# Four graph layers in FP32: first loads on one queue, identity products moved behind adj x, no warming products, planned times anew

## The chip, the cores and the metric

The kernel runs on one core of a Trainium2 chip. A core has five engines that each work through their own instructions in order and wait for one another by semaphores: PE (TensorE, matrix products), DVE (VectorE), ACT (ScalarE), POOL (GpSimd) and SP (SyncE), which here issues DMA transfers. The metric is the device time of one execution in microseconds (us). The profile comes from one execution that was recorded by the hardware profiler.

## The reference

The input x has 128 graphs of 128 nodes with 512 features, and adj is one 128x128 matrix. Four layers follow each other, each with a residual sum and a layer norm over the features. Cut to what matters:

```python
# layer 0
y = einsum('nm,bmd->bnd', adj, x);  x = norm(x + y @ w0 + bias0)
# layer 1
q, k, v = x @ Wq.T, x @ Wk.T, x @ Wv.T
rel = adj.T * einsum('bnd,bmd->bnm', q, k)
rel = rel / norm2(rel, axis=2);     x = norm(x + rel @ v)
# layer 2
h = x @ W;  e = leaky_relu(h @ a1 [:, :, None] + h @ a2 [:, None, :]) * adj
att = softmax(e);                   x = norm(x + elu(att @ h + beta * h))
# layer 3: both of its weights are adj, so that it needs max over d of (adj x), and b
A = einsum('od,bdn->bon', adj, x);  x = norm(x + relu(max(A, -1) + b))
```

All of it is in 32-bit floats.

## The kernel before, in words

**Tiling.** The 128 graphs are taken in 32 groups of four (G = 4, NG = 32). A group's x is one tile of 128 nodes by 4 by 512. Each group goes through `layer0` to `layer3`, and the groups overlap: while one is in layer 0, the group before is in layer 1 and an older one in layers 2 and 3.

**The names on PE.** Layer 0: `p_y` is adj x for one graph (four products of 128x128 into a PSUM bank, each two instructions in the records[...]), which ACT copies into yT. `r_y` is the product of yT with w0. Layer 1: `p_xT` transposes x, `r_m` multiplies it by m_qk (Wq and Wk were multiplied into one matrix at the start, `r_qk`), DVE adds the result up in tT, `p_rel` is tT times xT, `r_v` the product with Wv (transposed at the start by `p_wv`), `p_o` the product with the normed rel. Layer 2: `p_z` gathers by the attention, `r_z` multiplies by the weight. Layer 3: `p_a` is adj x again. `wa` makes rows of the weight times a, once.

**The four weighted products.** `product` replaces a 2x2 block product by seven block products (numbers 1 to 7). They need sums of blocks: POOL makes those of the left operand (`left_factors`: s_y, s_x, s_q), DVE makes those of the weight once (`weight_blocks`: t_0, t_k, t_m, t_v, t_2). The seven go into three PSUM regions: 1, 6, 7 and 4 share bank r0, 2 has a bank of tag pi, 5 and 3 share bank r12. After each of them `out(i)` reads the region (DVE adds it to the destination, or ACT copies it), and the next one of the same region accumulates on top. From the third group on, products 2 and 4 are split once more into small ones (the rows named `pi_`).

**Bias.** For `r_y` the bias is put into the bank ahead of the products: `fill` lets ACT write `bias_sb` into regions r0 and r12, and the products accumulate on it without a start flag. So that they accumulate, each of these two banks has to have been written once by PE. Two products of the identity (`first_r`, 128x512 each, four instructions together) do this at the very start.

**What sets the order.** There is no automatic scheduler. `emit(at, f)` files a piece of work under a planned time `at`, and at the end all pieces are sorted by it and issued; every engine then keeps its program order. Pieces of the steady groups have their times in `TABLE` (a slot per group), groups 0 and 1 have exceptions in `FIRST`, the last three groups in `LAST`; `STEPS` holds the offsets of the seven products and the small ones. One-time pieces have times of their own. All that goes through the order-keeping helper has line L26 in the profile.

**The start.** SP issues adj, x_0, x_1 (of group 0, 256 KB each), bias (broadcast to all partitions), x_2, x_3, wq, wk, wv, w2, a, beta, b3, while ACT issues w0 on its own queue (L110). The later x loads of a whole group (1 MB) are pieces. PE has, in this order: first_r, p_adjT (the transpose of adj), eight products `p_warm` of the identity that nobody reads (16 instructions), the four p_y of group 0, then r_y.

The lines that the change touches first:

```python
warm = bank("p_warm")
for i in range(WARM):
    pe.matmul(warm[:, :P], ident, ident, start=True, stop=True)
```

Of the kernel before, what the change touches and what calls it, by code (L numbers as in the profile page):

```python
# [8 lines left out]
FP = mybir.dt.float32  # L9
# [20 lines left out]
def kernel(  # L30
# [32 lines left out]
    nc = tc.nc  # L63
# [10 lines left out]
    WARM = 8  # L74
# [19 lines left out]
    nc.sync.dma_start(adj_sb, adj)  # L94
    x1, x2, x3 = {}, {}, {}

    def load(g):
        x1[g] = data.tile([P, G, D], FP, tag="x1", name=f"x1_{g}", bufs=3)
        if g == 0:
            for b in range(G):  # L100
                nc.sync.dma_start(x1[g][:, b, :], x[b])
                if b == 1:
                    nc.sync.dma_start(bias_sb, on_all(bias0, D))
        else:
            sync.dma_start(x1[g], x[g * G : (g + 1) * G].rearrange("b n d -> n b d"))

    bias_sb = const.tile([P, D], FP)
    load(0)
    w0_sb = const.tile([P, K, D], FP)
    nc.scalar.dma_start(w0_sb, w0.rearrange("(k p) f -> p k f", p=P))  # L110
    wq_sb = work.tile([P, K, D], FP, tag="tv", name="wq_sb")
    nc.sync.dma_start(wq_sb, wq.rearrange("(k p) f -> p k f", p=P))
    wk_sb = work.tile([P, K, D], FP, tag="c", name="wk_sb")
    nc.sync.dma_start(wk_sb, wk.rearrange("(k p) f -> p k f", p=P))
    wv_sb = work.tile([P, K, D], FP, tag="xB", name="wv_sb")
    nc.sync.dma_start(wv_sb, wv.rearrange("(k p) f -> p k f", p=P))

    w2_sb = const.tile([P, K, D], FP)
    nc.sync.dma_start(w2_sb, w2.rearrange("(k p) f -> p k f", p=P))
    a_sb = data.tile([P, 2, D], FP, tag="x3", name="a_sb", bufs=1)  # L120
    nc.sync.dma_start(a_sb.rearrange("p s d -> p (s d)"), on_all(a2, 2 * D))
    beta_sb = const.tile([P, 1], FP)
    nc.sync.dma_start(beta_sb, on_all(beta, 1))
    b3_sb = const.tile([P, 1], FP)
    nc.sync.dma_start(b3_sb, b3.rearrange("(p o) -> p o", o=1))
# [5 lines left out]

    for tag, n in (("r0", 1), ("r12", 1)):
        for i in range(n):
            r = psum.tile([P, 2, H], FP, tag=tag, name=f"first_{tag}_{i}", bufs=n)
            pe.matmul(r, ident, ident[:, None, :].to_broadcast([P, G, P]), start=True, stop=True)
# [7 lines left out]

    warm = bank("p_warm")
    for i in range(WARM):
        pe.matmul(warm[:, :P], ident, ident, start=True, stop=True)
# [99 lines left out]
    def row(at, step, n=G):  # L246
# [4 lines left out]
        load=[-21.1232], y=[0.9608, 1.8251, 2.1487, 2.7922],  # L251
        y_sums=[4.5561, 5.0639, 6.7629, 6.9969], y_inner=[5.2833, 7.5035, 7.9599, 7.7423],
        y_w=[6.4865, 10.1067, 9.7011, 18.5098, 16.5578, 25.5346, 18.8593],
        stats0=[13.0727, 13.9676, 15.6348, 14.8804], norm0=[15.6928],
        apply0=[16.441, 16.56, 17.1055, 18.4252], turn=[16.9531, 18.9169, 15.0983, 23.7872],
        turn_blocks=[17.6387, 18.378, 19.3199, 18.8892], move=[21.2268, 20.1475, 23.7935, 24.4105],
        x_sums=[25.5484, 25.8887, 25.5714, 27.1546], x_inner=[27.0248, 27.3651, 27.6181, 27.4647],
        m=[28.2059, 29.9451, 30.7559, 39.3743, 35.0579, 32.0807, 31.5941],
        scores=[35.5574, 36.2751, 36.3095, 39.6263], masked=[40.1785], squares=[41.2658],
        turn_rel=[40.8158], move_rel=[43.2987, 45.3105, 45.5881, 44.1661], inverse=[42.7358],  # L260
        v=[41.1537, 34.8028, 35.2269, 32.9135, 36.819, 44.1908, 45.5822],
        attend=[51.1788, 52.5818, 53.9439, 54.1297], residual=[51.7575, 52.9793, 54.8472, 55.5115],
        squares1=[52.1071, 55.1681, 55.5885, 56.295], dots=[52.6394, 54.6161, 55.8601, 56.5298],
        norm1=[56.6185], scale=[58.0637], apply1=[67.3359, 67.3118, 68.311, 67.3949],
        spread=[61.4852], leaky=[62.1614], weighted=[62.3481], greatest=[63.6868], exps=[63.9389],
        divide=[64.6743], turn_att=[66.48], with_beta=[55.7842], turn_blocks_2=[65.0697],
        move_2=[65.6032], gather=[70.1205, 71.0446, 73.2368, 74.4083],
        z_sums=[74.7466, 74.9675, 75.3471, 79.5091], z_inner=[76.2873, 76.452, 76.7576, 79.7843],
        z_w=[76.5238, 78.3454, 80.9549, 82.1806, 80.3108, 74.0925, 83.986],
        exp=[84.1886, 85.0555, 95.1779, 97.9857], elu=[86.5931, 86.915, 97.0853, 99.5009],  # L270
        norm2=[100.4793], apply2=[101.1271, 102.2, 101.6434, 101.6261],
        widen=[102.9021, 104.404, 104.6097, 106.3071],
        top=[104.9696, 105.5877, 105.8825, 107.7194], norm3=[108.5946],
        apply3=[109.0064, 110.4459, 109.9895, 111.6524], store=[116.2428],
# [4 lines left out]
            y=[-0.9173, 0.2561, 2.5559, 2.6098], y_sums=[5.7842, 6.1923, 7.6412, 8.0217],  # L279
            y_w=[6.656, 6.9826, 8.5177, 10.5158, 10.5177, 12.1185, 12.1169],  # L280
            stats0=[14.8567, 15.0593, 15.0036, 15.7551], norm0=[16.1054],
            m=[26.9197, 27.6264, 27.6652, 28.2251, 29.8853, 32.0185, 32.0172],
            scores=[35.9958, 37.3155, 38.45, 39.3155], masked=[39.5575], squares=[42.4727],
            turn_rel=[41.0869], move_rel=[42.4032, 42.1994, 41.3572, 41.7949],
            v=[42.7111, 44.0451, 45.3088, 46.3784, 47.3081, 48.2976, 49.1509],
            attend=[50.3341, 51.6935, 52.7247, 53.3341],
            residual=[51.2419, 52.2419, 52.8787, 54.4537],
            squares1=[51.6342, 53.6777, 54.5661, 54.7798], norm1=[56.2059],
            apply0=[17.374, 17.6244, 18.5295, 18.0555], turn=[18.8709, 19.7935, 20.9961, 21.5866],
            dots=[55.2805, 58.6316, 60.212, 60.5925], scale=[61.2871], spread=[61.7827],  # L290
            leaky=[62.1], weighted=[62.205], greatest=[64.0362], exps=[64.0854], divide=[65.2555],
            turn_blocks_2=[65.6], move_2=[67.0921],
        ),
        1: dict(
            y=[-11.6669, -10.4156, -10.312, -9.8874], y_sums=[-3.77, -3.67, -1.551, 3.0174],
            y_w=[7.0161, 7.9774, 8.126, 9.7685, 10.9791, 11.4015, 12.7041],
            stats0=[14.0438, 14.1814, 14.7308, 15.7036], norm0=[17.4806],
            attend=[49.1976, 51.8422, 53.416, 53.4184],
            apply0=[18.4423, 19.1027, 20.4894, 18.5104], turn=[21.0277, 21.0846, 21.3846, 21.542],
            x_sums=[22.8224, 24.281, 27.507, 28.0022],  # L300
# [5 lines left out]
            exp=[0.4623, 11.611, 13.6093, 21.9374], elu=[6.6028, 13.5806, 17.1367, 22.1806],  # L306
            norm2=[23.3538], apply2=[25.0389, 27.3987, 25.9338, 25.563],
            squares3=[35.4179, 39.239, 38.0926, 41.5412],
            widen=[44.4948, 56.0663, 55.0979, 58.4343], top=[44.9981, 56.3795, 60.4284, 60.9337],
            norm3=[62.9017], apply3=[64.4412, 66.5207, 68.7228, 67.9152], store=[69],  # L310
        ),
        NG - 2: dict(
            scale=[4.3047], apply1=[4.6775, 11.0377, 10.4618, 10.2756], spread=[6.9011],
            leaky=[8.5406], weighted=[8.6149], greatest=[11.14], exps=[12.7308], divide=[14.9407],
            turn_att=[19.4796], with_beta=[20.9256], gather=[33.1448, 34.2964, 34.1197, 33.8382],
            z_sums=[37.1312, 37.1799, 37.2299, 38.9411],
            z_w=[37.2, 39.2089, 40.5339, 42.6626, 45.9385, 46.5626, 47.9032],
            exp=[51.1816, 51.9016, 53.9016, 58.1278], elu=[51.9326, 54.0745, 59.5933, 63.8365],
            norm2=[65.6683], apply2=[66.9349, 67.9136, 68.7218, 69.9541],
            widen=[72.5885, 69.738, 73.9565, 76.7205], top=[73.9072, 73.9667, 75.9682, 78.4954],  # L320
            stats3=[68.0781, 73.1502, 70.7817, 73.9103], norm3=[73.9726],
            apply3=[81.0356, 88.4294, 88.4341, 88.4354], store=[91.3384],
        ),
        NG - 1: dict(
            load_w2=[-23.6669], m=[-1.0223, 1.0487, 2.4676, 3.6749, 7.9692, 8.2221, 9.9221],
            scores=[10.4191, 11.0622, 12.0436, 13.2103], masked=[14.918], squares=[15.9336],
            turn_rel=[17.0025], inverse=[19.5602],
            v=[17.0016, 19.283, 20.9796, 22.8356, 24.6364, 26.4739, 27.9989],
            attend=[30.1034, 30.2339, 30.8373, 30.4857],
            residual=[30.4, 31.4552, 33.8743, 31.7856],  # L330
            stats1=[33.7623, 34.1537, 33.9623, 34.1488], norm1=[34.3934],
            dots=[34.3979, 35.5481, 35.1904, 40.2755], scale=[40.5527],
# [87 lines left out]
    def by_columns(p, a, b, first):  # L420

        for c in range(2):
            for k in range(2):
# [21 lines left out]
    STEPS = {  # L445
        "m": (
            {
                1: (-1.2981, -0.3541),
                6: (1.724, 2.1528),
                7: (3.0677, 3.3979),  # L450
                5: (4.5184, 5.1615),
# [822 lines left out]
```

## Time and profile before

| what | value |
|---|---|
| median of three runs | 2141.93 us (2141.5 to 2142.24) |
| the profiled execution's own time | 2141.56 us |
| its span, first to last instruction | 2139.7 us |
| mean granted clock of PE | 0.997 |
| ACT busy, share of the span | 60% |
| POOL busy, share of the span | 45% |
| DMA, mean over the span | 65 GB/s |

How to read it: the span is shorter than the execution's time by 1.9 us, which lie before the first and behind the last instruction. The busy share of an engine is an average over the start, the steady groups and the end, which can have different limits. A row of the timeline gathers neighbouring instructions of one kind: its first number is the start of the first of them, its second the time to the end of the last; the ends of PE's instructions are modelled, so that starts are the safer numbers. A group takes about 65 us (the same p_rel of two neighbouring groups starts at 954.13 and 1019.09).

### The profile page before, as it was taken

Reading aid. Unit: us, or ns where it says so; the run is one execution under the profiler, and the core shown is the slowest. Engines: PE = TensorE matmul, PEld = TensorE weight load, DVE = VectorE, ACT = ScalarE, POOL = GpSimd, SP = SyncE. Lnnn points to the kernel's source line nnn. Section 1 sums busy time; section 2 is a strip of 40 time slices with the busy share of each in tenths; the row PEclk is TensorE's granted clock in tenths of the full one; section 3 lists DMA queues with packets and bytes.
Section 4 is the critical chain, followed back from the end, with each engine's and each line's share of the span. In section 5 each row is a group of like instructions: output and inputs, shape, how many; then the busy total and the mean of one; then the engine's idle time right before and its main releaser. Section 6 shows DMA issues by size and latency. Waiting matters only on the chain.

```text
span 2139.7 us, 36859 instructions
## 1 busy us (share of the span) xinstructions
PE 2116.7 (99%) x12325; PEld 1836.7 (86%) x12325; DVE 1725.1 (81%) x4961; ACT 1293.5 (60%) x2950; POOL 954.3 (45%) x949
## 2 busy tenths in 40 slices
PE   9999999999999999999999999999999999999996
PEld 7888888888888888888888888888888898888883
DVE  5688887878888878878878888788888788888777
ACT  3336556666566666567665566665666665676655
POOL 4244455444455444454444554444554444544431
PEclk9999999999999999999999999999999999999998
DMA  4012232221232222323222322212322213332201
GB/s 174 25 36 54 66 75 69 57 73 51 73 76 70 55 60 60 78 72 75 55 54 66 76 69 57 73 52 72 75 70 55 60 60 77 72 74 55 54 27 59
DMA packets 362524, 139.66 MB, mean 65 GB/s; under 512 B 303200, under 2 KB 318688, under 8 KB 362336
## 3 DMA queue, kind: packets, MB, share of 16 engines
q1 hardware_dynamic: 361808, 136.27, 24.9%
q8 instruction: 98, 1.61, 0.3%
q10 hardware_dynamic: 528, 1.05, 0.2%
q14 instruction: 90, 0.74, 0.1%
HBM read 56.17 MB, written 41.48 MB: 46 GB/s over the span
## 4 chain that ended last, share of the span: by engine, by line
PE 94%; DVE 3%; SPq 1%; DMA 1%; POOL 0%; issue 0%; ACT 0%; ACTq 0%; DVEq 0%; POOLq 0%
PE r_m L26 13%; PE r_y L26 13%; PE r_v L26 12%; PE r_z L26 12%; PE p_rel L26 5%; PE p_y L26 5%; PE p_o L26 5%; PE p_z L26 5%; PE p_a L26 5%; PE pi_m L26 4%; PE pi_y L26 4%; PE pi_z L26 4%; PE pi_v L26 4%; SPq L26 1%; DVE x L26 1%; DVE st L26 1%
## 5 line engine op out<-in xcount | busy, mean ns | idle before, releaser
L26 ACT ACTIVATE x<-x,nmean,rstd 128x512 f32<-128x512 f32 x384 | 285.7, 805 | 180.9 <-DVE nmean L26 180.9
L26 ACT ACTIVATE scr<-x 128x512 f32<-128x512 f32 x360 | 226.2, 628 | 73.3 <-DVE x L26 69.0
L26 POOL TENSOR_TENSOR rstd<-ve,mhalf 128x4 f32<-128x4 f32 (+1 forms) x99 | 98.7, 997 | 294.9 <-DVE ve L26 294.8
L26 DVE SCALAR_TENSOR_TENSOR scr<-x,wa 128x512 f32<-128x512 f32 x256 | 174.8, 683 | 4.6
L26 POOL TENSOR_TENSOR rn<-n,mhalf 128x4 f32<-128x4 f32 x32 | 32.7, 1023 | 307.4 <-ACT sq L26 307.4
L26 DVE TENSOR_TENSOR x<-r_y,x 128x512 f32<-128x512 f32 x194 | 129.3, 679 | 31.7 <-PE r_y L26 27.6
L26 DVE TENSOR_TENSOR c<-pi_z,c 128x128 f32<-128x128 f32 x420 | 123.5, 306 | 26.9 <-ACT c L26 18.4
L26 DVE SCALAR_TENSOR_TENSOR x<-p_o,rn,x 128x512 f32<-128x512 f32 x128 | 95.4, 745 | 58.4 <-PE p_o L26 58.1
L26 DVE TENSOR_TENSOR tT<-pi_m,tT 128x128 f32<-128x128 f32 x420 | 121.8, 305 | 22.3 <-PE pi_m L26 16.1
L26 ACT COPY r_y<-bias_sb 128x512 f32<-128x512 f32 x64 | 38.0, 593 | 161.4 <-DVE tT L26 161.3
L26 PE MATMUL p_z<-eT,x 128*128 128x128 f32 x1024 | 135.1, 275 | 0.3 <-DVE x L26 0.3
L26 POOL TENSOR_TENSOR s_x<-xT 128x512 f32<-128x512 f32 x64 | 80.6, 1280 | 121.5 <-DMA xT<-xB 73.1
L26 PEld LDWEIGHTS p_z<-eT,x 128*128 128x128 f32 x1024 | 129.2, 192 | 5.4 <-DVE x L26 1.3
L26 PE MATMUL p_a<-x,adjT 128*128 128x512 f32 x256 | 128.8, 607 | 5.1 <-ACT x L26 4.3
L26 PE MATMUL p_y<-adjT,x 128*128 128x128 f32 x1024 | 129.9, 275 | 0.5 <-DMA x<-in_x_dram 0.5
L26 PE MATMUL p_rel<-xT,tT 128*128 128x128 f32 x1024 | 129.8, 275 | 0.0
L26 ACT COPY yT<-p_y 128x512 f32<-128x512 f32 x128 | 74.8, 584 | 88.2 <-PE p_y L26 88.2
L26 PEld LDWEIGHTS p_y<-adjT,x 128*128 128x128 f32 x1024 | 124.5, 192 | 2.4 <-issue 0.7
L26 PEld LDWEIGHTS p_rel<-xT,tT 128*128 128x128 f32 x1024 | 124.7, 192 | 1.8
L26 PE MATMUL p_o<-v,relT 128*128 128x512 f32 x256 | 125.7, 594 | 0.3 <-ACT xT L26 0.2
L26 DVE TENSOR_TENSOR x<-pi_y,x 128x128 f32<-128x128 f32 x420 | 118.9, 300 | 6.3
L26 PE MATMUL r_m<-s_x,t_m 128*128 128x256 f32 x512 | 123.7, 384 | 0.0
(244 smaller groups left out, 6067.5 us busy)
## 6 DMA issues: line engine op xcount, KB each, us to landing
out_dram<-x SPq DMA_DIRECT2D x128, 256.0 KB, 2.0
x<-in_x_dram SPq DMA_DIRECT2D x31, 1024.0 KB, 7.7
xT<-xB SPq DMA_DIRECT2D x480, 64.0 KB, 2.3
relT<-relB SPq DMA_DIRECT2D x496, 16.0 KB, 1.8
eBd<-eB SPq DMA_DIRECT2D x30, 256.0 KB, 2.0
eT<-eBd SPq DMA_DIRECT2D x120, 64.0 KB, 1.9
s<-s2d SPq DMA_DIRECT2D x29, 256.0 KB, 5.1
w_sb<-in_L_gnn_weight_dram ACTq DMA_DIRECT2D x1, 1024.0 KB, 5.8
```

What stands on the lines that cost most here:

```text
L26: return lambda *args, **kw: self.tc.keep_in_program_order(op(*args, **kw))
```

## The change

1. All first loads go through SP, in the order adj, x_0 to x_3, bias, w0, wq, wk, wv, w2, a, beta, b3, and keep their program order.
2. The eight warming products are removed.
3. The two identity products move from the front into a piece of their own at 5.2287, behind the p_y of group 0; bias is filled in with the same lead (0.7) in group 0 as in most others (4.4 before).
4. Nearly all planned times are new. On PE this puts r_y of group 0 in the order 1, 6, 2, 7, 5, 4, 3 (before 1, 2, 6, 5, 7, 4, 3), r_m of group 0 in 1, 6, 5, 7, 2, 4, 3, with two p_wv pieces between its first and second product, and wa behind the last p_xT of group 1. In the steady groups it swaps four neighbours: r_m's second product stands ahead of a p_y, p_rel's first block ahead of two pairs of pi_m, one p_o behind two pairs of pi_z, another one later by a pair. On DVE, ACT and POOL neighbours change places in the same manner.

The diff, cut to its core:

```diff
-    WARM = 8
...
-    nc.sync.dma_start(adj_sb, adj)
+    sync.dma_start(adj_sb, adj)
...
             for b in range(G):
-                nc.sync.dma_start(x1[g][:, b, :], x[b])
-                if b == 1:
-                    nc.sync.dma_start(bias_sb, on_all(bias0, D))
+                sync.dma_start(x1[g][:, b, :], x[b])
...
     load(0)
+    sync.dma_start(bias_sb, on_all(bias0, D))
     w0_sb = const.tile([P, K, D], FP)
-    nc.scalar.dma_start(w0_sb, w0.rearrange("(k p) f -> p k f", p=P))
+    sync.dma_start(w0_sb, w0.rearrange("(k p) f -> p k f", p=P))
...
-    for tag, n in (("r0", 1), ("r12", 1)):
-        for i in range(n):
-            r = psum.tile([P, 2, H], FP, tag=tag, name=f"first_{tag}_{i}", bufs=n)
-            pe.matmul(r, ident, ident[:, None, :].to_broadcast([P, G, P]), start=True, stop=True)
...
-    warm = bank("p_warm")
-    for i in range(WARM):
-        pe.matmul(warm[:, :P], ident, ident, start=True, stop=True)
...
     TABLE = dict(
-        load=[-21.1232], y=[0.9608, 1.8251, 2.1487, 2.7922],
+        load=[-21.1232], y=[0.8907, 1.7114, 2.0872, 2.7307],
...
-        scores=[35.5574, 36.2751, 36.3095, 39.6263], masked=[40.1785], squares=[41.2658],
+        scores=[35.1374, 36.2751, 36.2963, 39.684], masked=[40.6138], squares=[41.0201],
...
         0: dict(
-            y=[-0.9173, 0.2561, 2.5559, 2.6098], y_sums=[5.7842, 6.1923, 7.6412, 8.0217],
-            y_w=[6.656, 6.9826, 8.5177, 10.5158, 10.5177, 12.1185, 12.1169],
+            y=[-1.7717, 0.0852, 3.1654, 1.6016], y_sums=[5.0471, 6.0029, 7.0582, 6.9775],
+            y_w=[6.681, 9.0756, 8.017, 10.1821, 10.0621, 11.6178, 11.6162],
...
-            m=[26.9197, 27.6264, 27.6652, 28.2251, 29.8853, 32.0185, 32.0172],
+            m=[26.0298, 29.7037, 27.4932, 28.0531, 29.6914, 32.2994, 32.0156],
...
-            lead={0: 4.4, 1: 0.2}.get(g, 0.7),
+            lead=0.7 if g != 1 else 0.2,
...
+    def write_banks():
+        for tag in ("r0", "r12"):
+            r = psum.tile([P, 2, H], FP, tag=tag, name=f"first_{tag}")
+            pe.matmul(r, ident, ident[:, None, :].to_broadcast([P, G, P]), start=True, stop=True)
+
+    emit(5.2287, write_banks)
-    weight_blocks([-2.4295, -1.7086, -1.5066, -1.4914], "0", w0_sb, inner_at=[29.9552, 28.8271])
-    weight_blocks([11.1091, 11.4933, 13.0971, 11.7463], "k", wk_sb, tag="x2")
+    weight_blocks([-1.8405, 5.9684, 8.7899, 8.7346], "0", w0_sb, inner_at=[30.413, 28.5062])
+    weight_blocks([12.2543, 13.8773, 19.4918, 12.5723], "k", wk_sb, tag="x2")
```

## The prediction

> **What bounds the kernel now.** I read the busy table of the page first, then PE's waits (columns: who waited for whom, us in all, times, longest). The first line is the page's, the other two are all that PE waited for between 130 and 2000 us.
> ```profile
> PE 2116.7 (99%) x12325; PEld 1836.7 (86%) x12325; DVE 1725.1 (81%) x4961; ACT 1293.5 (60%) x2950; POOL 954.3 (45%) x949
> PE pi_m L26 <- POOL si_x L26: 0.5, 1, 0.5
> PE pi_v L26 <- DVE v L26: 0.2, 1, 0.2
> ```
> Here 99% is no mean over unlike stages: for 1870 us PE waits 0.7 us in all. The change takes no matrix product out of this stretch, so its gain must lie before 130 us or at the end. PE's waits before 130 us are few:
> ```profile
> PE r_m L26 <- DVE tT L26: 0.9, 1, 0.9
> PE r_v L26 <- DVE x L26: 0.8, 1, 0.8
> PE r_y L26 <- DVE x L26: 0.8, 1, 0.8
> PE p_y L26 <- DMA x<-in_x_dram: 0.5, 1, 0.5
> PE p_xT L26 <- ACT xT L26: 0.3, 1, 0.3
> ```
> Then the timeline of the start (start, duration, engine, operation, count, idle time before it and its releaser):
> ```profile
> 1.36 3.78 PE L26 MATMUL first_r<-ident 128*128 128x512 f32 x4 [1.36 <-POOL ident masks.py:199]
> 4.93 0.42 PE L26 MATMUL p_adjT<-ident,adj_sb 128*128 128x128 f32 x1
> 5.15 2.40 PE L26 MATMUL p_warm<-ident 128*128 128x128 f32 x16
> 7.38 1.95 PE L26 MATMUL p_y<-adjT,x 128*128 128x128 f32 x16
> 9.88 2.02 PE L26 MATMUL p_y<-adjT,x 128*128 128x128 f32 x16 [0.54 <-DMA x<-in_x_dram]
> 11.73 3.62 PE L26 MATMUL r_y<-w_sb,yT 128*128 128x256 f32 x16
> ```
> first_r, p_adjT and p_warm fill PE until 7.38. That is about when its first x lands, by the DMA issues (size, us from issue to landing; issued at 0.73, 1.18 and 2.12):
> ```profile
> w_sb<-in_L_gnn_weight_dram ACTq DMA_DIRECT2D x1, 1024.0 KB, 5.8
> x<-in_x_dram SPq DMA_DIRECT2D x1, 256.0 KB, 5.7
> bias_sb<-in_L_gnn_bias_dram SPq DMA_DIRECT2D x1, 256.0 KB, 7.0
> ```
> So w0 lands at 6.5, the first x at 6.9 behind it, x_2 at 9.8 (it releases the second p_y), and the first weighted product r_y begins at 11.73.
>
> **What the Trainium skill says.** "TensorE: Matmul & The Clock Gate", Part 1: the array starts at half clock and is let up after a busy window of 3.41 us; the window runs free of the kernel. The trace agrees: first_r's instructions stand 0.85 us apart (weight loads at 2.38, 3.23, 4.08), a warm 128x512 one 0.43 (eight in 3.43, 2094.29 to 2097.72), and p_warm's 16 take 2.23 us where eight warm ones take 0.89: with c cold at 0.21 and the rest at 0.11, c is about 4, so the clock rises near 6.1 us. "DMA: Bandwidth & Descriptors", "Issuing engines are not separate DMA queues": all queues share 16 engines and interleave. Sharing is seen; here the first x did not interleave with w0 but came after it. "PSUM — Partial Sum Buffer", "The four PSUM rules": ScalarE's writes leave the accumulate bits alone, so the identity products must write a bank before ACT's fill of bias; they can be moved only as far as that. The trace shows the order (first_r at 1.36, the first fill by ACT at 9.85), not the bits.
>
> **The change part by part.**
> *Loads.* All stand on SP, adj first, then four x, bias, w0, wq. In the trace an issue costs SP about 0.45 us, and a full queue moves about 390 GB/s (a megabyte in 2.7 us). With 1 MB of w0 out of the way adj lands near 3.1 as now, the four x near 3.7, 4.4, 5.0 and 5.7 (0.65 each), bias near 7.3 (its slow stretch of about a microsecond kept), w0 near 10 instead of 6.5, wq near 12.5, wk near 15. From the ninth load SP holds each issue until the load eight before it has landed (now wk goes out at 6.56 as w0 lands, and a at 9.93 as x_2 does); wk will hang on adj, wv on the first x, and next group's x_1 on w0, so it lands near 26.3 against 13.77+13.0=26.8 now. Nothing else stands behind these on SP so early. Of the users, r_y needs w0 by about 11 (0 to 1 us of slack), r_qk wq and t_k wk by 24: hidden.
> *Start of PE.* p_adjT now waits for adj (3.1) instead of standing behind first_r; with its 0.42 product, DVE's copy (0.29) and two handovers, p_y starts near 4.1 instead of 7.38, and x keeps ahead of it. But nothing has warmed the array. 32 p_y instructions cost 6.7 us cold (0.21) and 3.57 warm (0.112). Counted from p_adjT at 3.2, the first full window of 3.41 us ends between 6.6 and 10.0. For the middle, 8.3, 20 instructions are cold (4.2) and 12 warm (1.34), and p_y ends near 9.7; for 6.6, 12 and 20, near 8.8; all cold, at 10.8.
> *Identity products.* Before, they cost nothing: they filled PE while x was on its way. Behind p_y they are on the path: 4x0.43=1.72 us warm. ACT's fill (0.59, and 0.26 from PE's end to a start) of the first bank runs beside the second product, so r_y starts 1.8 us after p_y's end: S=11.5 (10.6 to 12.8, the latter with some of first_r cold too) against 11.73. **Of 3.3 us of earlier start the cold clock and the moved products leave 0.2.** The removed warming products return nothing themselves, for they too ran under the wait for x.
> *Order of group 0.* From r_y at 11.73 to group 1's r_m at 94.17 are 82.44 us. PE's work there, by start to start: five sevens of r products at 1.727 (60.45), p_y and p_xT 3.57 each, p_wv 1.79, p_rel 3.57, wa 0.89, p_o 3.44, together 77.3. So 5.1 us are stalls: 1.2 in r_y, 2.1 up to group 1's r_y (58.45), 1.8 after. The new order has r_y's second product behind its first on the same bank: it waits for DVE's read (0.26+0.69+0.1=1.05), and the 0.78 before goes. In r_m two p_wv pieces stand between products of one bank, so the 0.9 goes; r_y of group 1 now ends on another bank than r_v begins with, so that 0.8 goes; wa covers ACT's copy ahead of p_o. I leave 1.05, 0.6 and 1.1: 2.7 of stalls, **2.4 less** (0.5 to 3 less). What is late next is DVE's sums of weight blocks (0.98 and 1.75 us for two of wk's beside a POOL sum, 0.69 alone); I can't place them to better than half a microsecond.
> *Steady groups.* On PE four neighbours change places, none adds or removes an instruction, and the period, 64.95 us now, stays PE's. The one that can bite is p_rel's first block, now two pairs of pi_m (4x0.11=0.45 us) earlier:
> ```profile
> 1018.17 0.69 DVE L26 TENSOR_TENSOR tT<-r_m,tT 128x512 f32<-128x512 f32 x1 [0.99 <-PE r_m L26]
> 1018.98 0.97 PEld L26 LDWEIGHTS p_rel<-xT,tT 128*128 128x128 f32 x8
> 1019.09 1.06 PE L26 MATMUL p_rel<-xT,tT 128*128 128x128 f32 x8
> ```
> tT ends at 1018.86, p_rel's loads begin at 1018.98. 0.45 us earlier the block's first products read rows of tT written before; only the third pair needs this one, and comes 0.45 later (4x0.112), which is just on time. I take 0, with a bound of 0.3 a group. Swaps on DVE, ACT and POOL cost nothing while PE's work covers them, as the two waits above show.
> *End.* From 2097 DVE is the chain (33.4 of the last 43 us busy). One c pair moves ahead of d (+0.25 at most), one wait for POOL's rstd (0.68, at 2101.97) loses its place on the chain (-0.6 at most): -0.4, bounds -1.2 and +0.4.
> *Sum* against the profiled execution (span 2139.7, run 2141.56): -0.2 -2.4 +0 -0.4 = -3.0, so 2138.6. The median shown, 2141.93, stands 0.37 above that execution, which lies inside the spread of the three; the forecast as a median is **2138.9**.
>
> **The rivals.**
> *B, the clock rises in its first window:* p_y ends near 8.8, S=10.6 (-1.1), and of the stalls only the 1.05 stays (-4.1): with the end's -0.4, -5.6, 2136.3. For it: the clock rose 4.7 us after the first product now. Against it: w0 lands only near 10, and DVE's first two sums of it (1.38) are needed for r_y's second product, so there is little behind 10.6 to win.
> *C, nothing gained:* p_y and part of first_r stay cold, S=12.8 (+1.1), and late weight sums on DVE leave half of the gain in stalls (-1.2): about 0, 2141.9. For it: the cold products must be run somewhere, and warming was what p_warm did. Against: the stalls named are two of one bank, which the order settles.
> *D, slower:* p_rel's third pair waits for DVE's tT in each steady group. The price is the wait, 29 times: 0.3 us gives +8.7, less the 3.0: +5.7, 2147.6. It decides from 0.25 us a group (0.25x29=7.3). For it: 0.1 us of margin. Against: the block's first four instructions need only rows of tT written a product earlier.
> *E, the change is not what it says:* its new planned times renumber the steady order and only the start differs in effect. That gives A's sum without the end, 2139.3.
>
> **How the numbers follow.** A (likeliest) 0.55, B 0.25, C 0.12, D 0.08. 0.2% is 4.3 us, about what a measurement of this kernel can tell from no change. A's own spread is -1.3 to -4.7, a tenth of it over the bound (0.05); B's is all over it: faster 0.30. A's rest and C: same 0.62. D: slower 0.08. The range runs from 2135.5, B with the end at its bound (-0.8 more), to 2143.2, C with the end's +0.4 and 0.03 us of D in each group.
>
> **What would show it.** Right: p_y's first row near 4.1 with 0.21 us from one instruction to the next, first_r between p_y and r_y, r_y near 11.5, r_m of group 1 near 91.5, a period of 64.95, no wait of PE over 0.5 us from 130 to 2000. Wrong: a wait p_rel <- DVE tT with 29 entries (D); p_y warm from its twelfth instruction and r_y near 10.6 (B); r_y past 12.5 or r_m of group 1 past 93.5 (C); a wait of r_y on w_sb would say that w0 is late; a period that differs by 0.1 us would outweigh all else.

## The result, and the profile after

The change made the kernel slower: 2153.17 us in the median of five runs (2149.21 to 2154.89) against 2141.76 (2141.5 to 2142.24), a ratio of 1.0052 with a 95% interval of 1.0037 to 1.0067. The forecast was 2138.9. Beside the median the scatter is new: the kernel before repeats within 0.8 us, the changed one within 5.7. The profiled execution, 2149.21, is the fastest of the five.

The page and PE's waits from 130 to 2000 us of the kernel after, the stretch that had 0.7 us of waits before:
```profile
span 2147.4 us, 36857 instructions
PE 2115.6 (99%) x12309; PEld 1832.4 (85%) x12309; DVE 1743.9 (81%) x4961; ACT 1298.5 (60%) x2950; POOL 954.0 (44%) x949
```
```profile
PE pi_m L26 <- DVE tT L26: 5.8, 8, 1.3
PE pi_m L26 <- POOL si_x L26: 0.9, 1, 0.9
```
PE's busy time fell by 1.1 us while the span grew by 7.7. The table names the wait that is new, but counts only the larger ones. By start to start of PE's rows, 14 of the steady groups lose something between r_m's product with t_m and the pi_m behind it, 8.3 us in all: four (7, 8, 22 and 23, the first group being 0) lose 1.45 each, eight lose 0.23 to 0.33, two under 0.1.

Where the 7.7 us lie, from the first r_m of the groups in the two traces (us, one execution of each kernel):

| stretch | before | after | difference |
|---|---|---|---|
| start to group 1's r_m | 94.17 | 92.83 | -1.3 |
| group 1's r_m to group 31's | 1946.0 | 1954.3 | +8.3 |
| group 31's r_m to the end | 99.5 | 100.2 | +0.7 |

A group in which nothing waits takes 64.86 us, 0.09 less than before, so the steady order also has something good in it, which the waits cover: about -2 us from group 1 to 31, as e12 will show (1944.0 against 1946.0).

PE's timeline of the start, kernel after, and its first DMA issues (KB each, us to landing):
```profile
2.65 0.45 PE L26 MATMUL p_adjT<-ident,adj_sb 128*128 128x128 f32 x1 [2.65 <-DMA adj_sb<-in_adj_dram]
4.16 6.47 PE L26 MATMUL p_y<-adjT,x 128*128 128x128 f32 x32 [1.07 <-DMA x<-in_x_dram]
10.47 1.88 PE L26 MATMUL first_r<-ident 128*128 128x512 f32 x4
12.79 1.96 PE L26 MATMUL r_y<-w_sb,yT 128*128 128x256 f32 x8 [0.44 <-DMA w_sb<-in_L_gnn_weight_dram]
15.79 1.97 PE L26 MATMUL r_y<-t,s_y 128*128 128x256 f32 x8 [1.03 <-DVE x L26]
```
```profile
x<-in_x_dram SPq DMA_DIRECT2D x4, 256.0 KB, 3.9
w_sb<-in_L_gnn_weight_dram SPq DMA_DIRECT2D x1, 1024.0 KB, 9.1
bias_sb<-in_L_gnn_bias_dram SPq DMA_DIRECT2D x1, 256.0 KB, 6.8
```
p_y starts 3.2 us earlier than before, but 23 of its 32 instructions run cold (0.21 us apart up to 9.5, then 0.11); r_y starts 1.1 us later than before, behind the landing of w0.

**Where a steady group loses its time.** The timeline of the kernel after at the new wait, first in a group that loses 1.45 us, then in one that loses nothing (POOL's first sum for s_y, the second x<-m of layer 2's elu on DVE, DVE's read of pi_m into tT, PE's next pi_m; the rows between them are left out):
```profile
490.19 1.26 POOL L26 TENSOR_TENSOR s_y<-yT 128x512 f32<-128x512 f32 x1 [2.41 <-ACT yT L26]
490.24 1.77 DVE L26 SCALAR_TENSOR_TENSOR x<-m,x 128x512 f32<-128x512 f32 x1
491.94 0.61 DVE L26 TENSOR_TENSOR tT<-pi_m,tT 128x128 f32<-128x128 f32 x2
492.60 0.49 PE L26 MATMUL pi_m<-si_x,u_m 128*128 128x128 f32 x2 [1.29 <-DVE tT L26]
...
622.52 0.69 DVE L26 SCALAR_TENSOR_TENSOR x<-m,x 128x512 f32<-128x512 f32 x1
623.04 1.30 POOL L26 TENSOR_TENSOR s_y<-yT 128x512 f32<-128x512 f32 x1 [2.98 <-ACT yT L26]
623.13 0.61 DVE L26 TENSOR_TENSOR tT<-pi_m,tT 128x128 f32<-128x128 f32 x2
624.00 0.38 PE L26 MATMUL pi_m<-si_x,u_m 128*128 128x128 f32 x2
```
The same DVE instruction takes 1.77 us where POOL's sum began 0.05 us ahead of it, and 0.69 where it began first. The read of pi_m stands behind it on DVE, and PE waits for that read. So it is in the four groups that lose 1.45 us (x<-m 1.66 to 1.77). In the eight that lose about 0.3, x<-m takes its 0.69 but begins 0.3 to 0.5 us later than in an undisturbed group, and the read behind it is late by as much. The kernel before, same place:
```profile
1008.85 0.61 DVE L26 TENSOR_TENSOR tT<-pi_m,tT 128x128 f32<-128x128 f32 x2
1010.16 0.69 DVE L26 SCALAR_TENSOR_TENSOR x<-m,x 128x512 f32<-128x512 f32 x1
1010.27 1.71 POOL L26 TENSOR_TENSOR s_y<-yT 128x512 f32<-128x512 f32 x1 [2.99 <-ACT yT L26]
1011.23 0.38 PE L26 MATMUL pi_m<-si_x,u_m 128*128 128x128 f32 x2
```
There the read comes ahead of the elu's second pair (x<-c and x<-m), 1.8 us before PE needs it. The race is nothing new: in 12 of the groups 3 to 30 of that trace x<-m began behind POOL's sum and took 1.57 to 1.77 us, and PE waited in none of them. In the code it is the second read of inner product 2 in `STEPS["m"]`: its offset went from 2.6924 to 3.4434, past the planned time of `elu[1]`.

This fits what the Trainium skill says in "SBUF — State Buffer", section "SBUF: two separate sides": DVE and POOL share a pair of ports as an exclusive lock, whoever of the two starts first has it for its whole instruction, and the other "fully blocks"; a DVE instruction with two operands in SBUF is concerned, against a POOL instruction that reads SBUF. The trace agrees in both directions: 0.69 against 1.77 for DVE, 1.27 against 1.71 for POOL. (tT<-pi_m, which reads PSUM, is not held up: 0.61 for two beside a running sum.)

### The profile page after: what moved, and what is told of

Read it like the earlier page. It is cut to its first block, busy times and chain, and to the rows that moved or that the text cites. A ratio compares the mean times of both kernels' runs of the same rounds, so it can differ in the third digit from the quotient of the medians.

```text
span 2147.4 us, 36857 instructions
## 1 busy us (share of the span) xinstructions
PE 2115.6 (99%) x12309; PEld 1832.4 (85%) x12309; DVE 1743.9 (81%) x4961; ACT 1298.5 (60%) x2950; POOL 954.0 (44%) x949
## 4 chain that ended last, share of the span: by engine, by line
PE 92%; DVE 5%; SPq 1%; DMA 1%; POOL 1%; ACT 0%; issue 0%; DVEq 0%; ACTq 0%; POOLq 0%
PE r_y L26 13%; PE r_v L26 13%; PE r_z L26 12%; PE r_m L26 11%; PE p_rel L26 5%; PE p_z L26 5%; PE p_o L26 5%; PE p_a L26 5%; PE pi_y L26 4%; PE pi_v L26 4%; PE pi_z L26 4%; PE pi_m L26 4%; PE p_y L26 4%; DVE x L26 2%; DVE scr L26 1%; PE r_qk L26 1%
## 5 line engine op out<-in xcount | busy, mean ns | idle before, releaser
L26 PE MATMUL p_o<-v,relT 128*128 128x512 f32 x256 | 131.1, 596 | 0.1
L26 DVE TENSOR_TENSOR v<-pi_v,v 128x128 f32<-128x128 f32 x420 | 120.8, 299 | 6.2
L26 PEld LDWEIGHTS r_z<-w_sb,s_z 128*128 128x128 f32 x496 | 94.1, 190 | 37.0 <-issue 25.7
```

Source lines behind the costliest of these rows:

```text
L26: return lambda *args, **kw: self.tc.keep_in_program_order(op(*args, **kw))
```

## The experiments

Each kernel was timed in 4 to 21 runs against the kernel before on the same chip (there 2141.7 to 2141.9 in the median).

| kernel | us, median | lowest to highest |
|---|---|---|
| e1, DVE's read put back | 2166.49 | 2165.2 to 2168.0 |
| e2, before with DVE's read late | 2144.84 | 2142.3 to 2146.4 |
| e3, before with the new start | 2151.33 | 2150.7 to 2151.6 |
| e4, e1 with the old start | 2167.33 | 2166.4 to 2171.4 |
| e5, DVE's and ACT's read put back | 2141.64 | 2139.9 to 2144.6 |
| e6, only ACT's read put back | 2156.33 | 2152.5 to 2158.1 |
| e7, e1 with the sum in four | 2148.73 | 2146.4 to 2149.5 |
| e8, before with both reads late | 2144.32 | 2143.2 to 2146.4 |
| e9, e5 with front and warming | 2141.77 | 2140.0 to 2143.6 |
| e10, e5 in groups 2 to 28 only | 2140.37 | 2138.7 to 2142.1 |
| e11, e10 with the old end | 2139.48 | 2138.4 to 2141.2 |
| e12, e11 in groups 2 to 30 | 2138.80 | 2137.4 to 2141.4 |

**e1: the DVE read put back, in the kernel after**
```diff
-                2: ((-0.7538, 1.5111), (2.2921, 3.4434), (3.9082, 4.7127)),
+                2: ((-0.7538, 1.5111), (2.2921, 2.6924), (3.9082, 4.7127)),
```


> The kernel after, with one DVE piece put back: the second read of pi_m (two tT additions) stands between the two elu pairs again, as in the kernel before; PE's order is untouched. Theory 1 (this one DVE swap makes PE wait): PE's waits pi_m <- DVE tT vanish, every steady period is the 64.86 us of the undisturbed groups of the kernel after (64.95 before, so 29 x 0.09 = 2.6 less), group 1's r_m stays at 92.8 (1.3 less), the end costs 0.7 more: 2141.8 - 3.2 = about 2138.6, with runs within 0.5 us of one another. Theory 2 (another moved piece is the cause, such as p_rel's earlier block): 2149 to 2155 as the kernel after, with the same scatter. Theory 3 (the new start sets a phase of the engines that makes the stalls): also 2149 to 2155.

2166.49, ratio 1.0116 (1.0102 to 1.0130): far slower than the kernel after, and no theory had that. The first theory, that this one swap is all, fell. The timeline of e1 shows why:
```profile
495.22 1.53 POOL L26 TENSOR_TENSOR s_y<-yT 128x512 f32<-128x512 f32 x1 [2.48 <-ACT yT L26]
495.73 1.57 DVE L26 SCALAR_TENSOR_TENSOR x<-m,x 128x512 f32<-128x512 f32 x1
497.40 0.63 ACT L26 ACTIVATE scr<-x 128x512 f32<-128x512 f32 x1 [1.64 <-DVE x L26]
498.03 1.05 ACT L26 COPY tT<-r_m 128x512 f32<-128x512 f32 x2
499.12 0.81 DVE L26 TENSOR_TENSOR tT<-pi_m,tT 128x128 f32<-128x128 f32 x3 [1.15 <-ACT tT L26]
499.99 0.38 PE L26 MATMUL pi_m<-si_x,u_m 128*128 128x128 f32 x1 [0.81 <-DVE tT L26]
```
With the read (two additions) ahead of it, x<-m now comes after POOL's sum in nearly every group. The wait for that read is gone, but ACT's second square (scr<-x) waits for x<-m, and the change has moved ACT's two copies of r_m into tT behind that square (`STEPS["m"]`, product 7, read 3.3979 to 4.2459). They come late, DVE's next additions to tT wait for them, and PE waits for these at the next pi_m: 0.7 us or more in 28 groups. In the two groups of this trace in which x<-m began first (19 and 28, 0.69 us) PE lost nothing there. Two reads were moved, on two engines, and each is dear only where x<-m is late, above all with the lost race.

**e2: only the DVE read late, in the kernel before**
```diff
-                2: ((-0.2439, 1.5111), (2.3325, 2.6924), (3.8348, 4.7127)),
+                2: ((-0.2439, 1.5111), (2.3325, 3.4434), (3.8348, 4.7127)),
```


> The kernel before, with one DVE piece moved as in the kernel after: the second read of pi_m behind both elu pairs; all else is the kernel before. Theory 1: PE waits pi_m <- DVE tT of 0.3 to 1.5 us in some of the groups, 7 to 13 us in all, 2149 to 2155 and scatter of some us. Theory 2 or 3: 2142 as before.

2144.84, ratio 1.0014 (1.0007 to 1.0020): slower and scattered, but by 3 us and not by 7 to 13. In its trace one group loses 1.46 us, with the signature of the kernel after, and seven lose 0.04 to 0.27:
```profile
1271.88 1.27 POOL L26 TENSOR_TENSOR s_y<-yT 128x512 f32<-128x512 f32 x1 [2.33 <-ACT yT L26]
1271.91 1.79 DVE L26 SCALAR_TENSOR_TENSOR x<-m,x 128x512 f32<-128x512 f32 x1
1273.63 0.61 DVE L26 TENSOR_TENSOR tT<-pi_m,tT 128x128 f32<-128x128 f32 x2
1274.29 0.49 PE L26 MATMUL pi_m<-si_x,u_m 128*128 128x128 f32 x2 [1.29 <-DVE tT L26]
```
The race was lost by 0.03 us here. In the undisturbed groups of e2, x<-m starts 0.63 us ahead of POOL's sum, in those of the kernel after 0.36 to 0.52.

**e3: only the new start, in the kernel before** (loads, no warming, identity products behind p_y, lead 0.7; old planned times)

> The kernel before with the new start alone: loads all on SP in order of need, no warming products, identity products behind p_y, fill with lead 0.7; all planned times are the old ones. Theory 1: r_y starts at 12.8 as in the kernel after (w0 lands at 12.7 and p_y is cold), 1.1 later than before; steady periods 64.95: about 2142 to 2143, no scatter. Theory 3 (phase): stalls in the steady groups and 2149 to 2155.

2151.33, ratio 1.0045 (1.0031 to 1.0059), and no new stalls in the steady groups (1946.4 from group 1 to 31, against 1946.0): the phase theory fell, and so did the 2142 to 2143 of the first. Nearly all of the loss is in the start; group 1's r_m comes at 103.13 instead of 94.17. The timeline:
```profile
12.91 1.60 DVE L26 TENSOR_TENSOR t<-w_sb 128x512 f32<-128x512 f32 x1 [9.41 <-DMA w_sb<-in_L_gnn_weight_dram]
13.92 1.72 POOL L26 TENSOR_TENSOR yT<-yT 128x512 f32<-128x512 f32 x1
14.55 1.64 DVE L26 TENSOR_TENSOR t<-t,w_sb 128x512 f32<-128x512 f32 x1
21.68 3.75 PE L26 MATMUL r_y<-t,s_y 128*128 128x256 f32 x8 [4.96 <-DVE x L26]
```
With w0 landing at 12.9, DVE's four sums of its blocks fall together with POOL's sums; the two take turns, 1.6 to 1.7 us each instead of 0.69 and 1.27, and DVE's read of the first r_y product stands behind them. In the kernel before w0 was there at 6.5, and these sums were done by 9.3, before POOL's first sum at 12.60. The new planned times, among them the order of `weight_blocks` and of r_y's products, are what makes the later w0 bearable: with them, the same start reaches group 1's r_m at 92.8 in the kernel after. Which of them does it was not tried alone.

**e4: e1 with the start of the kernel before**

> The kernel of e1 (new planned times, one read put back) with the start of the kernel before: w0 on ACT's queue, bias between x_1 and x_2, identity products at the front, eight warming products, lead 4.4. Theory 1: r_y starts at 11.7 instead of 12.8, what follows keeps the new order: 0.8 to 1.1 less than e1, 2137.5 to 2138. If the new loads help behind r_y (x_1, wk), it is not less than e1, 2138.6.

2167.33 against e1's 2166.49, ranges that overlap: no gain. r_y starts at 12.91 here too (the third p_y waits for x, and ACT's fill comes behind the copy of it), and group 1's r_m comes at 94.40, in e1 at 93.72. So with the new order of group 0 the old start is not better than the new one; differences under a microsecond are not settled by these runs.

**e5: both reads put back, in the kernel after**
```diff
-                7: (3.2489, 4.2459),
+                7: (3.2489, 3.3979),
...
-                2: ((-0.7538, 1.5111), (2.2921, 3.4434), (3.9082, 4.7127)),
+                2: ((-0.7538, 1.5111), (2.2921, 2.6924), (3.9082, 4.7127)),
```


> The kernel after with two reads put back to their places of before: DVE's second read of pi_m between the two elu pairs (as in e1), and ACT's two copies of r_m into tT ahead of the second square of the elu (in e1 that square, which waits for DVE's second x<-m, stood ahead of them). Theory 4 (DVE's second x<-m loses the race to POOL's first s_y sum and takes 1.6 to 1.8 us instead of 0.69; what stands behind it on DVE and ACT makes PE wait, so both reads have to be ahead): PE's waits pi_m <- DVE tT under 1 us in all although x<-m still takes 1.6 in most groups, periods 64.86, 2141.7 - 1.3 - 2.5 + 0.7 = about 2138.6, scatter under 1 us. Rival (yet another moved piece): 2149 or more.

2141.64, 11.5 us less than the kernel after; ratio to before 1.0000 (0.9992 to 1.0008). Undisturbed groups take 64.85 to 64.88, and one wait of 1.0 us is left from 130 to 2000. The race is still lost, and nobody waits any more:
```profile
1008.85 0.61 DVE L26 TENSOR_TENSOR tT<-pi_m,tT 128x128 f32<-128x128 f32 x2
1009.99 1.27 POOL L26 TENSOR_TENSOR s_y<-yT 128x512 f32<-128x512 f32 x1 [2.82 <-ACT yT L26]
1010.16 1.66 DVE L26 SCALAR_TENSOR_TENSOR x<-m,x 128x512 f32<-128x512 f32 x1
1010.95 0.39 PE L26 MATMUL pi_m<-si_x,u_m 128*128 128x128 f32 x2
```
It stays 3 us over the expectation. Its trace has 1.1 in group 1, where two more passes over x (scr<-x,wa) stand behind the read that was put back and ahead of the next one, 1.2 in group 29, 0.7 at the start (group 1's r_m at 93.53, not 92.8) and 0.3 at the end (100.6).

**e6: only ACT's read put back**

> The kernel after with only ACT's two copies of r_m put back ahead of the second square; DVE's read stays behind both elu pairs. Theory 4: the wait of the kernel after comes from the DVE read, not from ACT, so nothing is gained: 2149 to 2155 with the same scatter. Rival (ACT's order is the cause): 2139 to 2143.

2156.33, ratio 1.0066 (1.0052 to 1.0080): nothing gained, as expected, though a little above the range named. With e1 this says that either read alone is not enough.

**e7: e1 with POOL's first sum in four instructions**
```diff
-            pool.tensor_tensor(s1, blk(1, 0), blk(1, 1), ALU.add)
+            parts = 4 if inner_at is not None and name.startswith("y_") else 1
+            w = 2 * P // parts
+            for i in range(parts):
+                c = slice(i * w, i * w + w)
+                pool.tensor_tensor(s1[:, :, c], blk(1, 0)[:, :, c], blk(1, 1)[:, :, c], ALU.add)
```
(so in the steady groups' s_y only)

> The kernel e1 (2166) with POOL's first s_y sum of the steady groups cut into four instructions of 128x128 each; same result. Theory 4 (a running POOL instruction keeps DVE out until it ends): DVE's second x<-m waits for a quarter at most, 1.1 us instead of 1.6 to 1.8, PE's wait falls from 0.7 to 0.3 or less a group: 2147 to 2156. Rival (it is only ACT's order, POOL plays no part): 2166 as e1.

2148.73, 18 us less than e1, though POOL works more. PE's waits from 130 to 2000 us, e1 and then e7:
```profile
PE pi_m L26 <- DVE tT L26: 19.3, 26, 2.2
```
```profile
PE pi_m L26 <- DVE tT L26: 4.7, 10, 0.6
```
And the elu's second pair on DVE in e7:
```profile
1013.18 0.82 DVE L26 SCALAR_TENSOR_TENSOR x<-c,x 128x512 f32<-128x512 f32 x1
1014.10 0.76 DVE L26 SCALAR_TENSOR_TENSOR x<-m,x 128x512 f32<-128x512 f32 x1
```
x<-m falls from 1.57 to 0.76 (in groups 3 to 30 from 1.57 to 1.81, two excepted, to 0.75 to 0.83). ACT's order is that of e1, so POOL's long instruction, at the time at which it ran, is a necessary part. One thing is mixed in: two of the four parts need only earlier copies of yT and ran 1.3 us earlier, so that shorter locks and earlier work are not told apart.

**e8: both reads late, in the kernel before** (product 7 read at 4.2459 instead of 3.3979, and e2's edit)

> The kernel before with both reads late, as in the kernel after: DVE's read behind both elu pairs (e2, 2144.8) and ACT's copies of r_m behind the second square. Theory 4: the DVE wait of e2 stays, ACT's adds a little in the groups in which x<-m is late: 2145 to 2150, less than the kernel after loses, since x<-m starts 0.1 to 0.2 us earlier against POOL here. Rival (these two moves are all of it): 2153 + 2 = 2155.

2144.32, ratio 1.0012 (1.0005 to 1.0018): a little under the expected 2145 to 2150, no worse than e2, and far from the rival's 2155. So the two moves are necessary for the loss (e5) and not sufficient for all of it: in the kernel before they cost 2.4 us, in the changed one 11.5. What is added there is seen in the traces: in undisturbed groups DVE comes to the elu 0.1 to 0.3 us later against PE and POOL (its first x<-m starts 7.4 us after r_m in e2, 7.5 to 7.7 in the kernel after), for instance because a short mean<-mean,r now meets one of POOL's s_x sums and takes 0.89 us instead of 0.15. That this is the rest was not tried by a run of its own.

**e9: e5 with the identity products at the front and the warming products**

> The kernel e5 (both reads put back, 2141.6) with the identity products at the front again and the eight warming products; loads and all else as in e5. Theory W (r_y's start is set by w0, which lands at 12.7): p_y runs warm from 7.4 to 11, ACT's last copy is ready at 12, r_y still waits for w0 till about 12.8: 2141.6 within 0.5. Theory C (the cold p_y and the identity products set it): r_y at 11.9, 0.9 less, 2140.7.

2141.77 against e5's 2141.64: the time is that of theory W, the wait only in part. r_y starts at 12.80, as in the kernel after, but what ends its wait is ACT's fill; w0 had landed at 12.45:
```profile
12.80 1.99 PE L26 MATMUL r_y<-w_sb,yT 128*128 128x256 f32 x8 [1.17 <-ACT r_y L26]
```
With the loads in this order it does not matter where the identity products stand, nor whether PE was warmed: w0 holds r_y to 12.45 or later either way, and here the fill adds 0.35.

**e10, e11, e12: towards a version that beats both.** e10 puts the two reads back in groups 2 to 28 only; e11 has the end's planned times (`LAST`) of before as well; e12 puts the reads back to group 30.

> The kernel e5, but both reads are put back in groups 2 to 28 only; in groups 1, 29 and 30 they stay where the kernel after has them, since e5 shows a wait of 1.1 us in group 1 (its interval to group 2 is 62.71 against 61.63 in the kernel after) and one of about 1 us in group 29 (66.06 against 65.04). Theory 4: both waits go, 2.1 less than e5: 2139.5, 0.1% under the kernel before. If these waits have another cause: 2141.6.

> The kernel e10 with the planned times of the last three groups as in the kernel before. The end (from group 31's r_m to the last instruction) took 100.2 us in the kernel after and 99.5 before. If the new times of the end cost that: 0.7 less than e10, 2138.8. If the end is as good and the difference comes from how the groups before run into it: as e10, 2139.5.

> The kernel e11 with the two reads put back in groups 29 and 30 as well (2 to 30), where the trace of e11 shows one wait pi_m <- DVE tT of 1.4 us (group 29). With the old order of the end these groups stand as in the kernel before. Theory 4: that wait goes where it occurs, up to 1 us less than e11 in the median: 2138.5 to 2139.5, and less scatter. If putting back costs in group 29 what it cost in e5 (1.2): 2140.5.

e10: 2140.37, ratio 0.9993 (0.9985 to 1.0001); the waits of groups 1 and 29 are gone. e11: 2139.48, 0.9989 (0.9983 to 0.9996). Its step from e10 is within the scatter of the runs. In the two traces the end takes 100.1 and 99.2 us, but the group ahead of it 64.9 and 65.3; counted from group 30's r_m it is 165.0 and 164.5, so the new times of the end look 0.5 us worse, which the medians alone do not settle. e12: 2138.80, 0.9986 (0.9980 to 0.9993), faster than the kernel before by 3.0 us. In its trace x<-m loses the race in every group from 3 to 30, and it costs nothing. Of PE's waits from 130 to 2000 us one is left:
```profile
PE pi_m L26 <- POOL si_x L26: 0.6, 1, 0.6
```

## Why the prediction was wrong

**Steady groups: the step that failed.** "Swaps on DVE, ACT and POOL cost nothing while PE's work covers them, as the two waits above show." The two waits showed that the old order was covered, not by how much each read was ahead, and not that a moved one would be. Two of these swaps, DVE's read of pi_m and ACT's copies of r_m, cost 11.5 us (the kernel after against e5). The margin could be read in the trace of before: the read of pi_m ended at 1009.46 and PE's next pi_m began at 1011.23, 1.8 us, and the change put 1.4 us of elu between them, more if x<-m lost its race, which in that group began 0.11 us ahead of POOL's sum and in 12 others of that trace behind it. Read so, the swap leaves about 0.3 us and a chance of 1.5 us a group. I priced one PE swap (p_rel) in this manner and passed over those of the other engines as a group.

**Rival D** had the right side and form (PE waits on DVE's tT in steady groups, dear because it comes up to 29 times) and the wrong place: p_rel never waits in the trace after. Its price, 0.3 us in each group, was also of the wrong kind; here it is 1.45 us in four groups, about 0.3 in eight and next to nothing in the others, which fits the scatter. The four are among the groups in which the last DMA copy of xT lands latest (2.1 to 2.5 us ahead of r_m, the others mostly 2.6 to 3.8; the kernel before has 2.3 to 4.0): POOL's s_x and si_x sums then come into DVE's way, and DVE comes to the elu up to 0.9 us late. But groups 13, 14 and 19 lose 0.3 with copies that landed 3.2 us ahead or more, so this is not all of it; it is read from one trace, and no run tried it.

**Steady period.** Taken as unchanged; it fell by 0.09 us where nothing waits. A hiccup of 0.10 us between two pi_v that the kernel before had in each group is gone. The list of signs named the right lever ("a period that differs by 0.1 us would outweigh all else"); the sum had nothing for it.

**Loads.** The term of 390 GB/s, which gave 0.65 us for an x, was mis-sized. adj landed at 2.5 (3.1 predicted), the last x at 7.7 (5.7), bias at 9.8 (7.3), w0 at 12.7 (10). DMA moved 336 GB/s from 3 to 4.5 us, but 200 from 5 to 7.5, and 406 only from 9.5 on. The kernel before has such a slow stretch too (125 GB/s from 7 to 8), which the prediction kept at a microsecond and gave to bias; here it was longer and held up the x as well. What makes it is open. "r_y needs w0 by about 11 (0 to 1 us of slack)" fell with it. Two readings of the trace of before were off, without weight for the sum: from 5 to 6 us the first x did run beside w0 (0.23 MB on SP's queue, 0.16 on ACT's), and the issue of a at 9.93 stood behind the issue ahead of it (to 9.88), not behind x_2: its semaphore is that of x_1, which had landed at 7.6.

**Start of PE.** "p_y starts near 4.1": 4.16. That the cold clock and the moved identity products eat the earlier start was right. In nine traces with this start the step from 0.21 to 0.11 us comes between 6.8 and 9.8 us, where 6.6 to 10.0 was predicted; in the kernel after it comes at 9.5, after 23 cold instructions (20 for the middle), and p_y ends at 10.5 (9.7). From there 1.9 us of first_r lead to about 12.35; that r_y began at 12.79, at the end of my range, was w0's doing (0.44 us of wait). Both signs named for a late w0 came: r_y past 12.5, and its wait on w_sb. The warming products indeed returned nothing.

**Order of group 0.** From r_y to group 1's r_m 80.0 us, as predicted; the 1.03 wait of r_y's second product was predicted at 1.05. Part of that is luck: in this execution DVE's first weight sum began at 12.68, 0.01 us ahead of a POOL sum, and took 0.69 us. In the seven other traces with this start and order it took 0.86 to 1.79, the wait 1.21 to 2.13, and r_y to r_m 80.1 to 81.0. Group 1's r_m then lies between 92.44 and 93.80 over the eight, against 94.09 to 94.27 in three traces with the old start and order: with the late start the gain is 0.3 to 1.8, not 2.6. Not in the sum at all, and shown by e3: with the old planned times the new start alone costs 9.6 us.

**End.** -0.4 was predicted; the trace has +0.7, outside the bounds of -1.2 and +0.4. That the new times of the end are at fault fits e10 and e11 (0.5 us); which wait it is stays open.

**In sum**, the change without its two moved reads (e5) is worth nothing, 2141.64 against 2141.91. With the old times of the end as well, and the reads put back in groups 2 to 30 only (e12), it is worth -3.0 us. That this is the number forecast is luck: the forecast had -2.6 for the start, nothing for the steady groups and -0.4 for the new end, and e12's trace has -0.4, -2.0 and, with the old end, -0.4.

## What to carry to other kernels

A saturated engine hides what is behind the others only as far as each read is ahead of its reader: for a moved instruction on any engine, take the end of the read and the start of its reader from the trace, and put the moved work between them. Where DVE and POOL both work on SBUF, the length of a DVE instruction with two operands there is not a constant; look for pairs that start within some tenths of each other, and keep reads that free a PSUM bank ahead of them. A lost race costs nothing as long as no reader that PE needs soon stands behind it (e12). Cutting the long POOL instruction may help as well (e7, with the doubt named there). A load order "by need" has to count what is made from the data: w0 is needed by DVE's sums and not only by PE's first product with it (e3).

## What the runs showed of the hardware that was not expected

Which of DVE and POOL starts first decides who pays: x<-m took 0.69 us when it began 0.11 us ahead and 1.79 when it began 0.03 us behind, and POOL's sum 1.71 and 1.27. The edge is sharp. Of the 364 pairs in groups 3 to 30 of the 13 traces without e7's cut, x<-m took 0.69 us in all 145 in which it began ahead of the sum or at most 6 ns behind it, and 1.57 to 1.81 in all 219 in which it began 7 ns behind it or more.

When both have a row of sums, they alternate for as long as it lasts (e3: 1.6 to 1.7 each for some 8 us).

Scatter does not come from such a race alone. The kernel before has it open (12 groups of 28 lost) and repeats within 0.8 us, the kernel after, where PE hangs on it, within 5.7. But e12, whose trace shows no such wait, still spreads over 4.0 us in 21 runs; where from is open, though part may lie in the start, which differs by 1.4 us from trace to trace.
